# Four-layer graph network on one core: two of sixteen weight tiles of a unit move from VectorE to GpSimd

## The chip, the cores and the metric

The kernel runs on one core of a Trainium2 chip. A core has five engines with instruction queues of their own: TensorE (PE in the profile; its weight loads are PEld), VectorE (DVE), ScalarE (ACT), GpSimd (POOL) and SyncE (SP), which starts transfers. Each engine takes its instructions in order. SBUF is the working memory of 128 partitions, PSUM the memory in which TensorE leaves its sums.

The metric is the device time of one execution in microseconds (us). Before the change it is 1645.74, the median of 3 runs from 1645.39 to 1646.08.

## The reference, cut to what matters

The input is x (8 batches, N = 2048 nodes, 64 features) and one adjacency matrix of 2048 x 2048. Four layers follow, each x = layernorm(x + layer(x)). The first two are graph attention. For a batch, with h the projected features and s1, s2 two scores of every node:

```python
e = leaky_relu(s1[:, :, None] + s2[:, None, :], negative_slope=0.2)
att = softmax(where(adj > 0, e, very_small), axis=-1)
out = elu(matmul(att, h) [+ h in layer 0])
```

The third layer is the same with relu. The fourth takes a softmax along the neighbours for each feature.

A leaky relu is a maximum of two lines, and a factor that all weights of a row share drops out of a softmax. So in the first two layers the kernel needs no exponential of the 2048 x 2048 matrix. The weight of neighbour j for node i is, up to factors of i or of j alone, max(exp(0.8 s1[i]), exp(-0.8 s2[j])) times the mask; the factor exp(s2[j]) goes into the features of j.

## The kernel before

**Units.** A unit is one layer of one batch, named layer_batch. The first two layers run as 0_0 to 0_3, 1_0 to 1_3, 0_4 to 0_7, 1_4 to 1_7; then come the eight units of layer 2 (list `todo`, L1224). Layer 3 runs as background work.

**A unit's main loop** (L1297 to L1325) has K = 16 steps jb, one for each block of 128 neighbours. `attend` (L899) makes a weight tile w of 128 neighbours by 2048 nodes, and TensorE multiplies it in four chunks of 512 nodes with the features of that block, summing in the two PSUM tiles `acc`. In the first two layers the tile is one VectorE instruction, the maximum of a row and a scalar per partition, times the mask:

```python
dve.scalar_tensor_tensor(w, s.r, s.e[:, 1, jb : jb + 1], edge[:, jb, :], ALU.max, ALU.mult)
```

`edge` is the mask, 16 blocks of 128 x 2048 in fp8, kept in SBUF for the whole kernel. Tiles w share four buffers (tag "w").

**The row** s.r holds exp(0.8 s1) of all nodes, the same in each partition. Only unit 0_0 has it as f32 in SBUF. In the other 15 (`in_psum`, L566), `rows_term` (L569) splits the row on GpSimd into three bf16 pieces whose sum is the row (five small instructions on tile rT), writes them to DRAM, `prepare` (L724) loads them as r3, and `spread` (L744) has TensorE sum them into a PSUM tile r with four matmuls against ones. There is one such PSUM tile, so those matmuls come behind VectorE's last tile of the unit before. GpSimd does not read PSUM in this kernel.

**Background.** What a unit leaves to do, and what later units need, is written as generators (streams). After each step jb, `bg.step()` (L1325) takes every stream one step further; a stream says with the number that it yields how many steps it lets pass. Four of them matter here:
- `finish` (L937): ScalarE copies acc; TensorE multiplies it back to rows of nodes (p_o); VectorE takes the reciprocals of the sums (den); ScalarE scales (o); in layer 0 GpSimd adds hb; then eh and o on ScalarE and GpSimd (o<-o,eh is GpSimd's last sum), the statistics st_x (two VectorE reductions, and a power on GpSimd that takes isw_x to st_x), and x on ScalarE.
- `scores` (L677): from the new x to the scores of the next layer (p_xT, p_s), and the row.
- `features0` (L588): projection and layernorm of a batch for layer 0 (xs, p_h, st_h, y, h), and the row.
- `mean_pieces` (L552): the mean of all features in bf16 pieces, for nodes without neighbours, by small VectorE instructions (mean).

**Order.** The class InOrder (L68) keeps every engine in program order, the order in which Python writes the instructions. So a tile of the main loop and a background instruction written ahead of it on the same engine never change places, and an instruction that waits holds up all behind it. All such instructions carry line L78 in the profile; they are told apart by tile names. The buffers of a tag are handed out in the order in which they come free.

**The start.** Unit 0_0 also loads the adjacency matrix and makes the mask block by block (`load_raw`, L263; `mask`, L278). Eight of the blocks pass through buffers of tag "w", the others in halves through four buffers of tag "raw".

Of the kernel before, what the change touches and what calls it, by code (L numbers as in the profile page):

```python
# [8 lines left out]
F32 = mybir.dt.float32  # L9
BF16 = mybir.dt.bfloat16  # L10
U8 = mybir.dt.uint8
FP8 = mybir.dt.float8e4
I32 = mybir.dt.int32
AF = mybir.ActivationFunctionType
ALU = mybir.AluOpType
AX = mybir.AxisListType

P = 128
# [30 lines left out]
def gnn4_kernel(ctx: ExitStack, tc: tile.TileContext, t, out):  # L49
    nc = tc.nc  # L50
    x_in, adjT = t["x"], t["adjT"]
    B, N, F = x_in.shape
    K = N // P
# [8 lines left out]
    small = ctx.enter_context(tc.tile_pool(name="small", bufs=2))  # L62
    tmp = ctx.enter_context(tc.tile_pool(name="tmp", bufs=1))
    dram = ctx.enter_context(tc.tile_pool(name="dram", bufs=2, space=bass.MemoryType.DRAM))
# [40 lines left out]
    class Banks:  # L105
# [4 lines left out]
        pool = None  # L110
# [28 lines left out]
    pe, dve, act, pool = (InOrder(e) for e in (nc.tensor, nc.vector, nc.scalar, nc.gpsimd))  # L139
# [56 lines left out]
    work = ctx.enter_context(tc.tile_pool(name="work", bufs=2))  # L196
    early_ = ExitStack()
    early = early_.enter_context(tc.tile_pool(name="early", bufs=3))
# [49 lines left out]
    edge = consts.tile([P, K, N], FP8, name="edge")  # L248
# [14 lines left out]
    def load_raw(jb):  # L263

        if jb in AT_W:
            r = work.tile([P, N], I32, tag="w", name=f"raw_{jb}", bufs=4)
            nc.sync.dma_start(r, adjT[jb * P : (jb + 1) * P])
            raws[jb] = [r[:, : N // 2], r[:, N // 2 :]]
        elif jb < K:
            raws[jb] = []  # L270
            for h in range(2):
                r = early.tile([P, N // 2], I32, tag="raw", name=f"raw_{jb}_{h}", bufs=4)
                nc.sync.dma_start(
                    r, adjT[jb * P : (jb + 1) * P, h * (N // 2) : (h + 1) * (N // 2)]
                )
                raws[jb].append(r)
# [289 lines left out]
    def in_psum(layer, b):  # L566
        return layer < 2 and (layer, b) != (0, 0)

    def rows_term(sc, p, n, layer, b):  # L569

        if in_psum(layer, b):
            r = small.tile([K, P], F32, tag="rT", name=f"rT_{n}", bufs=1)
            act.copy(r, p)
            r3 = small.tile([K, 3, P], BF16, tag="rT3", name=f"rT3_{n}", bufs=1)
            for i in range(3):
                pool.tensor_copy(r3[:, i], r)
                if i < 2:
                    pool.tensor_tensor(r, r, r3[:, i], ALU.subtract)
            sc.row = dram.tile([3, K, P], BF16, tag="row3_d", name=f"row3_d_{n}", bufs=B + 1)
            nc.sync.dma_start(sc.row.rearrange("m k p -> k m p"), r3)  # L580
            return
        rT = small.tile([K, P], F32, tag="rT", name=f"rT_{n}", bufs=1)
        act.copy(rT, p)
        sc.row = dram.tile([K, P], F32, tag="row_d", name=f"row_d_{n}", bufs=B + 1)

        (nc.scalar if n == "0_0" else nc.sync).dma_start(sc.row, rT)
# [137 lines left out]
    def prepare(layer, b):  # L724

        n = f"{layer}_{b}"
        sc = S[layer, b]
        if in_psum(layer, b):
            sc.r3 = work.tile([P, 2 * N], BF16, tag="row", name=f"row3_{n}")[:3, :N]
            nc.sync.dma_start(sc.r3, sc.row.rearrange("m k p -> m (k p)"))  # L730
            sc.v = early.tile([P, K, F], F32, tag="pv", name=f"pv_{n}", bufs=2)
            pool.tensor_tensor(sc.v, V[layer, b].v, bc_f(sc.e[:, 2]), ALU.mult)
            return
        sc.r = work.tile([P, N], F32, tag="row", name=f"row_{n}")
        (nc.scalar if n == "0_0" else nc.sync).dma_start(
            sc.r, bass.AP(tensor=sc.row.tensor, offset=sc.row.offset, ap=[[0, P], [1, N]])
        )
        if layer < 2:
            sc.v = early.tile([P, K, F], F32, tag="pv", name=f"pv_{n}", bufs=2)
            pool.tensor_tensor(sc.v, V[layer, b].v, bc_f(sc.e[:, 2]), ALU.mult)  # L740
        else:
            sc.v = V[layer, b].v
# [147 lines left out]
    def exponential(b, chunk):  # L890
# [5 lines left out]
        )  # L896
        ahead[b, jb, c] = e

    def attend(u, jb, last):  # L899

        s = u.s
        if u.layer < 2:
            w = work.tile([P, N], F32, tag="w", name=f"w_{u.n}_{jb}", bufs=4)
            dve.scalar_tensor_tensor(
                w, s.r, s.e[:, 1, jb : jb + 1], edge[:, jb, :], ALU.max, ALU.mult
            )
        else:
            w = ahead[u.b, jb]
            if jb + 2 < K:
                clamp(u.layer, u.b, jb + 2)  # L910
            for c in range(2):
                sl = slice(c * 1024, (c + 1) * 1024)
                dve.tensor_tensor(w[:, sl], ahead[u.b, jb, c], edge[:, jb, sl], ALU.mult)
                chunk = 2 * jb + c + 2
                if chunk < 2 * K:
                    exponential(u.b, chunk)
                elif (u.b + 1, 0) in ahead:
                    exponential(u.b + 1, chunk - 2 * K)
        if jb == K - 1:
            last()  # L920
        sums = [u.acc[c // 2][F * (c % 2) : F * (c % 2) + F, :] for c in range(NCH)]
        for c in range(NCH):
            pe.matmul(
                sums[c],
                lhsT=s.v[:, jb, :],
                rhs=w[:, c * 512 : (c + 1) * 512],
                start=(jb == 0),
                stop=False,
            )
        if jb == K - 1:  # L930

            assert s.whole
            for c in range(NCH):
                rows = slice(32 * c, 32 * c + 3)
                pe.matmul(sums[c], lhsT=s.mean[rows], rhs=emptyT[rows], start=False, stop=True)
# [329 lines left out]
    for n, (layer, b) in enumerate(todo):  # L1265
        if (layer, b) == (2, 1):
            early_.close()
            late = ctx.enter_context(tc.tile_pool(name="late", bufs=1))
            bg.add(l3_products())
        if (layer, b) == (2, 5):  # L1270
            bg.add(flags())
        u = unit(layer, b)
        now[0] = layer
        nxt = todo[n + 1] if n + 1 < len(todo) else None
        done = nxt is None

        def first_exponentials():
            for chunk in range(2):
                if nxt is not None and nxt[0] == 2 and (nxt[1], 0) in ahead:
                    if (nxt[1], 0, chunk) not in ahead:  # L1280
                        exponential(nxt[1], chunk)

        def handover():

            if not done or nxt is None or S[nxt].__dict__.get("begun"):
                return
            if in_psum(*nxt):
                if n == 0:
                    Banks.use("psR", 1)
                spread(*nxt)  # L1290
            elif nxt == (2, 0):
                Banks.use("psE", 2)
                Banks.share()
            S[nxt].begun = True
            first_exponentials()

        for jb in range(K):  # L1297
            if n == 0:
                while masks < min(K, 9 + jb):
                    mask(p_deg, masks)  # L1300
                    masks += 1
                    if masks == K:
                        empties(p_deg)
            attend(u, jb, handover)
            if jb == K - 1:
                end = [lambda u=u: finish(u)]
                if layer < 2:
                    end += [2 if now[0] < 2 else 1, lambda layer=layer, b=b: scores(layer + 1, b)]
                else:
                    end += [1, lambda b=b: l3_features(b)]  # L1310
                if layer == 1 and b % NB == NB - 1:
                    end += [lambda b=b: group(b // NB)]
                bg.add(chain(*end), begun=True)
            elif not done and jb >= 10 and ready(*nxt):
                prepare(*nxt)
                done = True
            if done and nxt is not None and nxt[0] == 2 and jb >= K - 2:
                clamp(*nxt, jb - (K - 2))
            if layer == 0 and jb == 2 and 6 <= b + 4 < B:
                load_x(b + 4)  # L1320
            if n == 0 and jb == 3:
                bg.add(constants())
            if layer == 0 and jb == 4 and 2 <= b + 2 < B:
                bg.add(features0(b + 2))
            bg.step()  # L1325
        while not done:
            bg.step()
            if ready(*nxt):
                prepare(*nxt)
                done = True  # L1330
                if nxt[0] == 2:
                    clamp(*nxt, 0)
                    clamp(*nxt, 1)
        handover()
# [508 lines left out]
```

## Time and profile before

The span in the profile is 1643.8 us. Busy times of the whole span:

| engine | busy us | share |
|---|---|---|
| PE | 1349.0 | 82% |
| DVE | 1301.1 | 79% |
| ACT | 802.8 | 49% |
| POOL | 823.7 | 50% |
| PEld | 667.2 | 41% |

The 15 units in question run from 102.4 to 838.8 us. A line of a group reads: source line, engine, operation, output<-inputs, sizes, count | busy us, mean ns of one | idle time of the engine just before such instructions, and what ended it. A line of a timeline reads: start us, length us, engine, line, operation, output<-inputs, sizes, count, and in brackets the idle time before it and its releaser. "issue" means that the profile shows no wait. Instructions of one group that follow each other are merged, so `x4` with 9.10 us is four tiles.

### The profile page before, as it was taken

The numbers are of one execution on the slowest core, as the hardware profiler recorded it, in microseconds if no ns is written. First come the engines' busy times: TensorE is split into PE (matmuls) and PEld (weight loads), VectorE is DVE, ScalarE is ACT, GpSimd is POOL, SyncE is SP. The second block draws the span as 40 slices with busy tenths as digits, with TensorE's granted clock in tenths as the row PEclk, the third lists the DMA queues.
The fourth block names the chain that finished last, engine by engine and source line by source line (L and its number), as shares of the span: only waits on it lengthen the run. The fifth ranks groups of instructions, "written<-read, shape, count | busy, mean of one in ns | idle before, by whom it ended". The sixth has DMA issues, their size and how long they took to land.

```text
span 1643.8 us, 20952 instructions
## 1 busy us (share of the span) xinstructions
PE 1349.0 (82%) x8162; PEld 667.2 (41%) x8162; DVE 1301.1 (79%) x1334; ACT 802.8 (49%) x1635; POOL 823.7 (50%) x726
## 2 busy tenths in 40 slices
PE   3687879888888898888887676699896999587996
PEld 2222323333333343233322231165452545476885
DVE  4888877899887989898888878969897977738444
ACT  5234664443265443442378857676656664242111
POOL 2145353422222454321257748877789877546332
PEclk9999988899998999999999878899998999888998
DMA  8800000000000000000000000000010000000000
GB/s 329 215 5 1 1 2 1 1 2 1 1 1 2 1 2 2 2 1 26 26 1 26 26 1 27 0 26 8 30 33 7 4 4 11 10 4 14 11 14 19
DMA packets 42190, 36.86 MB, mean 22 GB/s; under 512 B 37509, under 2 KB 37813, under 8 KB 39906
## 3 DMA queue, kind: packets, MB, share of 16 engines
q1 hardware_dynamic: 41538, 34.26, 6.8%
q8 instruction: 66, 1.08, 0.3%
q10 hardware_dynamic: 544, 1.17, 0.2%
q14 instruction: 42, 0.34, 0.1%
HBM read 30.94 MB, written 4.45 MB: 22 GB/s over the span
## 4 chain that ended last, share of the span: by engine, by line
PE 31%; DVE 17%; ACT 7%; POOL 4%; issue 3%; POOLq 0%; DVEq 0%; ACTq 0%
PE p_l L78 18%; PE acc L78 11%; DVE w L78 10%; ACT e L78 3%; DVE o L78 2%; DVE st_x L78 2%; DVE x L78 1%; POOL v L78 1%; PE p_o L78 1%; ACT x L78 1%; POOL vf L78 1%; DVE f L78 1%; PE p_s L78 1%; POOL w L78 1%; POOL o L78 1%
## 5 line engine op out<-in xcount | busy, mean ns | idle before, releaser
L78 PE MATMUL acc<-w,pv 128*64 128x512 f32 x2048 | 525.4, 642 | 117.0 <-DVE w L78 95.1
L78 DVE SCALAR_TENSOR_TENSOR w<-r,se,edge 128x2048 f32<-128x2048 f32 x240 | 551.9, 2340 | 27.1 <-PE r L78 26.3
L78 PEld LDWEIGHTS <-edge 128*128 128x128 fp8e4 x3842 | 321.2, 99 | 153.1 <-issue 94.3
L78 PE MATMUL p_l<-v,edge 128*128 128x256 bf16 x3072 | 351.1, 275 | 37.4 <-ACT nd L78 13.1
L78 PE MATMUL acc<-w,x 128*64 128x512 f32 x1024 | 281.8, 667 | 87.4 <-DVE w L78 79.9
L78 ACT ACTIVATE e<-w,s_g 128x1024 f32<-128x1024 f32 x256 | 277.6, 1113 | 148.1 <-DVE w L78 103.7
L78 DVE TENSOR_TENSOR w<-e,edge 128x1024 f32<-128x1024 f32 x256 | 300.3, 1214 | 56.3 <-ACT e L78 54.2
L78 PEld LDWEIGHTS acc<-w,pv 128*64 128x64 f32 x2048 | 134.9, 143 | 401.6 <-issue 199.5
L78 POOL TENSOR_SCALAR w<-row,hi_g,lo_g 128x2048 f32<-128x2048 f32 x128 | 270.5, 2118 | 37.6 <-PE acc L78 33.4
L78 PEld LDWEIGHTS acc<-w,x 128*64 128x64 f32 x1024 | 64.0, 146 | 231.9 <-DVE w L78 154.7
L78 POOL TENSOR_TENSOR eh<-eh,x 128x1024 f32<-128x1024 f32 (+2 forms) x24 | 36.5, 1533 | 153.2 <-ACT eh L78 153.2
L78 ACT ACTIVATE nd<-p_l,empty 128x256 f32<-128x256 f32 x64 | 30.1, 470 | 158.8 <-PE p_l L78 158.8
L78 ACT ACTIVATE x<-o,st_x 128x64 f32<-128x64 f32 x256 | 87.4, 432 | 26.9 <-DVE st_x L78 26.9
L78 ACT COPY oT<-acc 128x512 f32<-128x512 f32 x48 | 25.7, 587 | 122.6 <-PE acc L78 122.5
L78 ACT ACTIVATE o<-p_o,den 128x64 f32<-128x64 f32 x256 | 56.2, 323 | 48.5 <-DVE den L78 48.4
L78 DVE RECIPROCAL den<-p_o 128x4 f32<-128x4 f32 x96 | 16.9, 179 | 73.5 <-PE p_o L78 59.5
L78 POOL TENSOR_TENSOR st_h<-isw_h,mhalf 128x16 f32<-128x16 f32 x8 | 23.6, 2956 | 99.2 <-DVE isw_h L78 94.9
L78 PEld LDWEIGHTS p_o<-rh,oT 128*128 128x128 f32 x384 | 51.2, 200 | 53.5 <-issue 32.0
L78 POOL TENSOR_TENSOR st_x<-isw_x,mhalf 128x16 f32<-128x16 f32 x24 | 70.5, 2936 | 2.0
L78 PE MATMUL p_o<-rh,oT 128*128 128x130 f32 x384 | 64.0, 302 | 7.9 <-ACT o L78 5.6
L78 POOL TENSOR_SCALAR isw<-isw 128x4 f32<-128x4 f32 x32 | 8.5, 265 | 122.6 <-DVE isw L78 122.5
L78 DVE TENSOR_REDUCE st<-sq 128x4 f32<-128x256 f32 x32 | 13.2, 414 | 70.4 <-ACT sq L78 70.3
(233 smaller groups left out, 1511.5 us busy)
## 6 DMA issues: line engine op xcount, KB each, us to landing
raw<-in_adjT_dram SPq DMA_DIRECT2D x8, 1024.0 KB
raw<-in_adjT_dram SPq DMA_DIRECT2D x16, 512.0 KB
row<-rows_d_g SPq DMA_DIRECT2D x8, 1024.0 KB
x<-in_x_dram SPq DMA_DIRECT2D x8, 512.0 KB
out_dram<-o SPq DMA_DIRECT2D x64, 64.0 KB
row<-row_d ACTq DMA_DIRECT2D x1, 1024.0 KB
row_d<-rT SPq DMA_DIRECT2D x15, 12.0 KB
row<-row_d SPq DMA_DIRECT2D x15, 12.0 KB
```

Of the source, the lines that this page charges most:

```text
L78: ins = f(*args, **kwargs)
```

## The change

In each of the 15 units, GpSimd makes the tiles 4 and 9 in place of VectorE, by a maximum and a product on each half of a tile. For this the change
- writes the f32 row to DRAM too (`sc.row1`) before it is split, and keeps the rest of the splitting in a tile of its own, rT1, so that the row isn't overwritten;
- loads that row into SBUF in `prepare`, in two halves that are the same in each partition (`sc.r1`);
- keeps bf16 copies of the mask blocks 4 and 9 (`wide`), made by VectorE after the last two steps of unit 0_0;
- renames the buffers of the half blocks: in place of four of tag "raw" two each of "half0" and "half1", which the row halves and the mask copies take over later;
- writes the tile three steps ahead: at jb = 1 tile 4, at jb = 6 tile 9, in the same four buffers of tag "w".

It is for taking work from VectorE to an engine that is busy for less of the span.

```diff
@@ load_raw
-                r = early.tile([P, N // 2], I32, tag="raw", name=f"raw_{jb}_{h}", bufs=4)
+                r = early.tile([P, N // 2], I32, tag=f"half{h}", name=f"raw_{jb}_{h}", bufs=2)
@@ rows_term
             act.copy(r, p)
+            sc.row1 = dram.tile([K, P], F32, tag="row_d", name=f"row_d_{n}", bufs=B + 1)
+            nc.sync.dma_start(sc.row1, r)
+            q = small.tile([K, P], F32, tag="rT1", name=f"rT1_{n}", bufs=1)
             r3 = small.tile([K, 3, P], BF16, tag="rT3", name=f"rT3_{n}", bufs=1)
             for i in range(3):
-                pool.tensor_copy(r3[:, i], r)
+                pool.tensor_copy(r3[:, i], q if i else r)
                 if i < 2:
-                    pool.tensor_tensor(r, r, r3[:, i], ALU.subtract)
+                    pool.tensor_tensor(q, q if i else r, r3[:, i], ALU.subtract)
@@ prepare
+            sc.r1 = []
+            for h in range(2):
+                r = early.tile([P, N // 2], F32, tag="half0", name=f"row1_{n}_{h}", bufs=2)
+                nc.sync.dma_start(
+                    r,
+                    bass.AP(
+                        tensor=sc.row1.tensor,
+                        offset=sc.row1.offset + h * (N // 2),
+                        ap=[[0, P], [1, N // 2]],
+                    ),
+                )
+                sc.r1.append(r)
@@ attend
+    BY_POOL = (4, 9)
+    wide = {}
+
+    def by_pool(u, jb, h):
+        s = u.s
+        if h == 0:
+            ahead[u.n, jb] = work.tile([P, N], F32, tag="w", name=f"w_{u.n}_{jb}", bufs=4)
+        sl = slice(h * (N // 2), (h + 1) * (N // 2))
+        w = ahead[u.n, jb][:, sl]
+        pool.tensor_scalar(w, s.r1[h], s.e[:, 1, jb : jb + 1], None, ALU.max)
+        pool.tensor_tensor(w, w, wide[jb][:, sl], ALU.mult)
+
     def attend(u, jb, last):
 
         s = u.s
-        if u.layer < 2:
+        if in_psum(u.layer, u.b) and jb + 3 in BY_POOL:
+            for h in range(2):
+                by_pool(u, jb + 3, h)
+        if (u.n, jb) in ahead:
+            w = ahead[u.n, jb]
+        elif u.layer < 2:
@@ main loop
             attend(u, jb, handover)
+            if n == 0 and jb >= K - 2:
+                j = BY_POOL[jb - (K - 2)]
+                wide[j] = early.tile([P, N], BF16, tag="half1", name=f"wide_{j}", bufs=2)
+                dve.tensor_copy(wide[j], edge[:, j])
```

## The prediction

> **What bounds the kernel now.** I read the page first. Its groups name the two costs that the change touches: the VectorE instruction that makes a weight tile, and the TensorE instructions that use it.
>
> ```profile
> L78 PE MATMUL acc<-w,pv 128*64 128x512 f32 x2048 | 525.4, 642 | 117.0 <-DVE w L78 95.1
> L78 DVE SCALAR_TENSOR_TENSOR w<-r,se,edge 128x2048 f32<-128x2048 f32 x240 | 551.9, 2340 | 27.1 <-PE r L78 26.3
> ```
>
> 240 tiles are 15 units of 16; a tile costs VectorE 2.34 us, and TensorE's idle time ahead of it is mostly a wait for VectorE (95.1 us of 117.0). Next I cut the trace into the 15 units that the change reaches (from the first r matmul of one to that of the next; 102.4 to 838.8 us) and asked for busy times by window. Columns: span, then busy us of PE, PEld, DVE, ACT, POOL, clock, DMA.
>
> ```profile
> 211.30:266.50 55.20, 45.29 (x189) 18.93 (x189) 44.96 (x35) 30.07 (x98) 22.64 (x23) 0.78 0.00 1
> 409.50:457.40 47.90, 40.28 (x181) 14.39 (x181) 40.89 (x27) 11.01 (x31) 9.58 (x6) 0.93 0.00 1
> 558.70:608.00 49.30, 47.94 (x441) 21.75 (x440) 42.08 (x35) 22.95 (x75) 26.10 (x25) 0.93 0.01 2
> sum 736.40, PE 625.27 PEld 239.70 DVE 633.18 ACT 326.03 POOL 257.69; mean PE 41.68 PEld 15.98 DVE 42.21 ACT 21.74 POOL 17.18
> ```
>
> A unit lasts 49.1 us on average with PE busy 41.7 and DVE 42.2: neither is the bound throughout. Which one ends a wait is seen in the instructions of one unit, 1_3 (409.5 to 457.4), DVE first, PE after it:
>
> ```profile
> 419.52 9.10 DVE L78 SCALAR_TENSOR_TENSOR w<-r,se,edge 128x2048 f32<-128x2048 f32 x4
> 432.23 0.18 DVE L78 RECIPROCAL den<-p_o 128x4 f32<-128x4 f32 x1 [3.61 <-issue]
> ...
> 437.27 1.26 DVE L78 SCALAR_TENSOR_TENSOR mean<-mean,later,mean 128x64 f32<-128x64 bf16 x1
> 438.45 4.60 DVE L78 SCALAR_TENSOR_TENSOR w<-r,se,edge 128x2048 f32<-128x2048 f32 x2
> 442.97 1.20 DVE L78 TENSOR_REDUCE st_x<-o 128x16 f32<-128x1024 f32 x1
> ```
>
> ```profile
> 426.14 5.35 PE L78 MATMUL acc<-w,pv 128*64 128x512 f32 x16
> 431.42 1.16 PE L78 MATMUL p_o<-rh,oT 128*128 128x130 f32 x8
> ...
> 440.84 1.94 PE L78 MATMUL acc<-w,pv 128*64 128x512 f32 x8 [1.50 <-DVE w L78]
> ...
> 446.48 1.94 PE L78 MATMUL acc<-w,pv 128*64 128x512 f32 x8 [1.45 <-DVE w L78]
> 450.36 7.07 PE L78 MATMUL acc<-w,pv 128*64 128x512 f32 x24 [1.94 <-DVE w L78]
> ```
>
> In the first half VectorE makes tiles 3 to 6, then stands 3.61 us in front of the reciprocal, whose p_o TensorE makes only at 431.42, after tiles 4 and 5: TensorE is late there. In the second half TensorE waits for tiles (1.50, 1.45, 1.94 us), so VectorE is late, up to tile 15 and the r matmul behind it. **Tile 4 lies in the half where VectorE has time to spare, tile 9 at the start of the half where it has none.**
>
> **What the Trainium skill says.** (1) "GPSIMD Engine Reference", 3.1: a two-input tensor_tensor of 2048 f32 takes 4497 ns on GpSimd, 1.96 times VectorE. The trace agrees: o<-o,eh, 1024 elements, takes 2361 ns. (2) "SBUF — State Buffer", "SBUF: two separate sides": VectorE (in a two-port mode, or with two SBUF inputs) and GpSimd take a shared port pair for a whole instruction, and the other blocks. The trace agrees on both sides. The mean instruction above takes 1.26 us beside eh<-eh,x; its usual time is 0.28. And in unit 0_0, whose row is in SBUF, tiny GpSimd instructions take the length of a tile:
>
> ```profile
> 93.34 0.28 POOL L78 CAST rT<-rT 16x128 bf16<-16x128 f32 x1
> 93.71 2.35 POOL L78 TENSOR_TENSOR rT<-rT,rT 16x128 f32<-16x128 f32 x1
> ```
>
> The tiles of the other 15 units read r from PSUM and so have one SBUF input: all 240 took 2315 to 2352 ns, whatever GpSimd did. So the big instructions won't collide with the new work; small ones will. (3) "VectorE: DVE Perf Modes", "Mode 2×_2P": a copy within SBUF can yield two elements a cycle; the wide copies have no row of their own, and the mask row (edge<-raw, 1024 elements in 689 ns) points the same way.
>
> **The change, part by part.** *Removed:* 2 x 2.34 = 4.68 us of VectorE a unit, 70.2 us in 15. *Added on GpSimd:* per tile, two halves of a max and a product. The max: clamp rows (w<-row,hi_g,lo_g) have median 2.05 us for 2048, so 1.02 a half. The product f32 x bf16: between 2.10 (vf<-vf,v, 4203 ns for 2048) and 2.36 (o<-o,eh). A tile is 6.2 to 6.8 us; I take 6.7, the high end, because the product has o<-o,eh's layout. That is 13.4 us a unit, 201 in all, on an engine busy 17.2 of 49.1: it fits as a sum, so the question is what queues behind it. *Added elsewhere:* one 8 KB write and two 512 KB loads a unit, hidden (the DMA engines are at 0.01, and the loads stand behind the r3 load that matters); 0_0's own 1 MB row held VectorE 10.1 us, and w4 is needed 20 us after the new load in 0_1. The renamed halves keep the four buffers. The f32 row q adds no instruction.
>
> *Order of the queues.* by_pool(4) is written at jb 1, by_pool(9) at jb 6, each ahead of what the streams add in the same step; how many steps a stream lets pass is the number that it yields, and GpSimd's order in the trace is the same. Buffers of tag w go round in the order in which they come free; with w4 and w9 written early, w4 waits for the unit before's w13, w9 for w2, w6 for w3, w7 for w4. By the times of before w9 can start when PE is through w2 (421.2 in 1_3) and be done 6.7 us later, well before 440.8; and PE is through w3 at 423.8, before VectorE would start w6. No tile is late for lack of a buffer.
>
> *Tile 4:* in 1_1, 1_2, 1_3, 1_4, 1_5, 1_6, 0_5, 0_6, 0_7 its 2.34 us become more idle time ahead of a reciprocal or of st_x<-o, whose input comes from TensorE, ScalarE and GpSimd: nothing. In 0_1 and 0_2 about 0.6 and 0.3. In 0_4 and 1_7 VectorE has no such wait left (1.1 us of slack), so part counts.
>
> *Tile 9:* I listed for every unit how long after VectorE ended a tile TensorE began it. Where that stays near 0.1 us from tile 10 to 15, TensorE has only its idle time to lose and the unit ends 2.3 us sooner, less what the reductions then wait. In 1_3 VectorE would be at st_x<-o at 440.6, but o<-o,eh ends at 441.06: 1.9. So: 1_1 2.3, 1_2 2.2, 1_3 1.9, 1_4 2.3, 1_5 2.3, 1_6 1.9 = 12.9. 0_4 and 1_7, both tiles, limited by the idle time that TensorE has from tile 4 on (2.8 and 3.7 us) and by the reduction: 2.5 + 2.8 = 5.3. 0_5 0.5, 1_0 0.5 (TensorE runs 3 us behind). With 0_1 and 0_2: 12.9 + 5.3 + 1.0 + 0.9 = **20.1 us gained**.
>
> *Delays behind GpSimd.* The queue is in program order, and VectorE waits for it in order:
>
> ```profile
> 592.40 1.22 DVE L78 TENSOR_REDUCE st_x<-o 128x16 f32<-128x1024 f32 x1 [3.49 <-POOL o L78]
> ```
>
> ```profile
> 590.01 2.35 POOL L78 TENSOR_TENSOR o<-o,eh 128x1024 f32<-128x1024 f32 x1
> ```
>
> In 0_6, by_pool(9) comes in after o<-o,hb (ends 578.8) and ends 585.5; the rT, h and eh instructions queue behind it and o<-o,eh ends 595.4, not 592.4: 3 us, of which TensorE's lag later takes 0.5. In 0_3 it falls between eh<-eh,x (ends 235.5) and o<-o,eh, which starts at 242.2, not 238.4; VectorE's next tile, for which TensorE already waited 4.31 us, comes 3 us later. In 0_7 eh<-eh,x waits 2.2, of which 0.9 arrives. In 1_2 and 1_5 the power of st_x ends some 2 us later and holds VectorE 0.6 and 0.5. Sum 2.5 + 3.0 + 0.9 + 1.1 = **7.5 us lost**.
>
> *The shared port.* I laid the 6.7 us windows over VectorE's small instructions with two SBUF inputs: 14 meetings, 6 of them in the half that VectorE sets. A meeting costs on average what is left of a GpSimd instruction: (1.02² + 2.36²)/(2 x 3.38) = 0.98, say 0.9 us; **5.4 us lost**.
>
> *The wide copies:* two in 0_0, before the first tile of 0_1. 1.3 us each from the mask row, at most a tile's 2.34; 0.79 and 1.19 us of idle time follow. 0.6 to 2.7; I take **1.0 us**.
>
> Net 20.1 - 7.5 - 5.4 - 1.0 = 6.2 us: 1645.7 - 6.2 = **1639.5**.
>
> **The rivals.** *GpSimd's queue becomes the bound* (slower). Then a product or two stands ahead of a chain in all eight units that finish a first-layer unit (0_1, 0_2, 0_3, 1_0, 0_5, 0_6, 0_7, 1_4), 3 us each as in 0_6, 24 in all; and of the 8 meetings in the first halves half count too, 5.4 + 4 x 0.98 = 9.3. With the copies 24 + 9.3 + 1.0 - 20.1 = +14: 1660. For it: 78% more work on a queue that VectorE waits for in order. Against: in 1_1, 1_2, 1_3, 1_5 and 1_6 GpSimd stands idle 15 to 33 us at a time ahead of eh, and in 0_1 and 0_2 13 to 23 us. *Washed out:* gain and delays cancel, 1645. *VectorE was the bound after all:* both tiles count, down to TensorE's floor. VectorE then gives 70 us, less the reciprocals' waits in the first halves, about half: 1611. For it: the 95.1 us wait; against: 3.61 us of idle VectorE right behind tile 6.
>
> **How the numbers follow.** Forecast 0.48, slower rival 0.30, washed out 0.14, both tiles 0.08. Faster is forecast plus both tiles, with a little taken off because 6 us is near 3.3: 0.55. Slower 0.32, within 0.2% 0.13. The range must leave out most of the extremes: from 1624 (the 20.1 us without any loss) to 1660 (the middle of the slower rival).
>
> **What would show it.** Right: GpSimd busy 257.7 + 201 us in these units; TensorE's wait for VectorE's w shorter in second halves; reciprocals waiting longer by tile 4; o<-o,eh about 3 us later in 0_3 and 0_6. Wrong: big VectorE tiles longer than 2352 ns; GpSimd's halves over 3.4 us; TensorE waiting for w from POOL, which would mean that a buffer or the row came late; or a reduction waiting for POOL o in units where I put no delay.

## The result, and the profile after

The changed kernel takes **1674.71 us**, the median of four runs (1673.27 to 1676.72), against 1645.57 us before (1644.35 to 1646.08). The ratio is 1.0179, with a 95% interval from 1.0161 to 1.0197: slower by 1.8%, where 0.4% faster was forecast, and above the range of 1624 to 1660.

The group of the matmuls on the page of the changed kernel, whose line of before the prediction shows:

```profile
L78 PE MATMUL acc<-w,pv 128*64 128x512 f32 x2048 | 526.3, 647 | 144.1 <-DVE w L78 118.1
```

The tiles and the new work, in the groups of the changed kernel with different shapes kept apart:

```profile
L78 DVE SCALAR_TENSOR_TENSOR w<-r,se,edge 128x2048 f32<-128x2048 f32 x210 | 483.9, 2338 | 25.9 <-PE r L78 23.6 <-PE acc L78 2.3
L78 POOL TENSOR_SCALAR w<-row,hi_g,lo_g 128x2048 f32<-128x2048 f32 x128 | 269.9, 2114 | 36.2 <-PE acc L78 27.3 <-issue 2.5 <-DVE vf L78 2.4
L78 POOL TENSOR_SCALAR w<-row,se 128x1024 f32<-128x1024 f32 x60 | 170.6, 2843 | 23.8 <-PE acc L78 23.7
L78 POOL TENSOR_TENSOR w<-w,wide 128x1024 f32<-128x1024 f32 x60 | 128.0, 2133 | 5.0
L78 DVE TENSOR_REDUCE st_x<-o 128x16 f32<-128x1024 f32 x24 | 29.2, 1215 | 60.0 <-POOL o L78 60.0
```

VectorE lost 30 tiles, as meant, and each remaining tile keeps its length (2338 ns, 2340 before). The product takes 2133 ns, inside the bounds of the prediction. The max (w<-row,se) takes **2843 ns for half a tile**; 1020 had been assumed. The clamp in the second line, which does two operations and handles twice the elements, takes 2114. A tile thus costs GpSimd 2 x (2.84 + 2.13) = 9.95 us instead of 6.7, and TensorE's idle time behind VectorE's w rose from 95.1 to 118.1 us where it should have fallen.

The last line says where the tiles' work arrives. The first reduction of a layernorm waits 60.0 us for GpSimd's o. In the waits (who waits for whom: total us, times, longest) of before the same wait is small:

```profile
DVE st_x L78 <- POOL o L78: 10.7, 6, 3.6
```

After the change:

```profile
DVE st_x L78 <- POOL o L78: 60.0, 14, 12.3
```

Unit 0_6 holds the longest. It starts at 571.9 us in the trace of the changed kernel. On GpSimd:

```profile
590.69 2.37 POOL L78 TENSOR_TENSOR o<-o,hb 128x1024 f32<-128x1024 f32 x1 [1.93 <-ACT o L78]
593.04 2.84 POOL L78 TENSOR_SCALAR w<-row,se 128x1024 f32<-128x1024 f32 x1
595.96 2.14 POOL L78 TENSOR_TENSOR w<-w,wide 128x1024 f32<-128x1024 f32 x1
598.07 2.85 POOL L78 TENSOR_SCALAR w<-row,se 128x1024 f32<-128x1024 f32 x1
601.01 2.13 POOL L78 TENSOR_TENSOR w<-w,wide 128x1024 f32<-128x1024 f32 x1
...
608.40 2.34 POOL L78 TENSOR_TENSOR eh<-eh,x 128x1024 f32<-128x1024 f32 x1
610.82 2.34 POOL L78 TENSOR_TENSOR o<-o,eh 128x1024 f32<-128x1024 f32 x1
```

On VectorE, and below it on TensorE, in the same stretch:

```profile
589.56 11.36 DVE L78 SCALAR_TENSOR_TENSOR w<-r,se,edge 128x2048 f32<-128x2048 f32 x5
613.19 1.22 DVE L78 TENSOR_REDUCE st_x<-o 128x16 f32<-128x1024 f32 x1 [12.27 <-POOL o L78]
614.33 2.34 DVE L78 SCALAR_TENSOR_TENSOR w<-r,se,edge 128x2048 f32<-128x2048 f32 x1
```

```profile
616.73 5.65 PE L78 MATMUL acc<-w,pv 128*64 128x512 f32 x12 [6.65 <-DVE w L78]
```

Tile 9 is ready at 603.1 and late for nobody. But the 10 us that it takes stand in GpSimd's queue ahead of eh and o. VectorE, after five tiles in one piece, stands 12.27 us in front of the reduction, and behind that reduction stands its next tile, for which TensorE then waits 6.65 us. o<-o,eh ends 41.2 us after the start of the unit, 33.7 before the change.

Cut at the start of each unit, the 15 units took 736.4 us before and 765.3 after, +28.9, which is nearly the whole difference. The largest losses are in 0_6 (+7.8), 0_7 (+6.9), 1_0 (+4.9), 1_5 (+3.5) and 1_2 (+3.4). Units 1_3, 1_6 and 1_1 gained 3.6, 1.9 and 0.6.

### The profile page after: what moved, and what is told of

Its sections match the earlier page's. It is cut to its first block, busy times and chain, and to the rows that moved or that the text cites. A ratio compares the mean times of both kernels' runs of the same rounds, so it can differ in the third digit from the quotient of the medians.

```text
span 1672.5 us, 21160 instructions
## 1 busy us (share of the span) xinstructions
PE 1348.2 (81%) x8162; PEld 667.9 (40%) x8162; DVE 1260.5 (75%) x1306; ACT 801.6 (48%) x1635; POOL 1121.0 (67%) x846
## 4 chain that ended last, share of the span: by engine, by line
PE 29%; DVE 15%; ACT 8%; POOL 7%; issue 3%; POOLq 0%; DVEq 0%; ACTq 0%
PE p_l L78 17%; PE acc L78 10%; DVE w L78 8%; ACT e L78 3%; POOL w L78 2%; DVE o L78 2%; DVE st_x L78 1%; POOL o L78 1%; DVE x L78 1%; POOL v L78 1%; ACT x L78 1%; PE p_o L78 1%; POOL vf L78 1%; ACT o L78 1%; POOL st_x L78 1%
## 5 line engine op out<-in xcount | busy, mean ns | idle before, releaser
L78 PE MATMUL acc<-w,pv 128*64 128x512 f32 x2048 | 526.3, 647 | 144.1 <-DVE w L78 118.1
L78 DVE SCALAR_TENSOR_TENSOR w<-r,se,edge 128x2048 f32<-128x2048 f32 x210 | 483.9, 2338 | 25.9 <-PE r L78 23.6
L78 POOL TENSOR_SCALAR w<-row,se 128x1024 f32<-128x1024 f32 x60 | 170.6, 2843 | 23.8 <-PE acc L78 23.7
L78 POOL TENSOR_TENSOR w<-w,wide 128x1024 f32<-128x1024 f32 x60 | 128.0, 2133 | 5.0
L78 DVE TENSOR_REDUCE st_x<-o 128x16 f32<-128x1024 f32 x24 | 29.2, 1215 | 60.0 <-POOL o L78 60.0
```

The lines of the kernel that those rows point to most:

```text
L78: ins = f(*args, **kwargs)
```

## The experiments

All ratios are against the kernel before on the same chip (1647.2 to 1648.0 us). "In us" means (ratio - 1) x 1645.6, the interval in the same way.

**1. Does the length of the max set the time?** Three kernels have the same 60 halves in the same places and differ only in how long a half's max takes. One repeats the max:

```diff
-        pool.tensor_scalar(w, s.r1[h], s.e[:, 1, jb : jb + 1], None, ALU.max)
+        k = s.e[:, 1, jb : jb + 1]
+        pool.tensor_scalar(w, s.r1[h], k, k, ALU.max, ALU.max)
```

> The maximum is written with two operations (max, max with the same scalar) like the clamp of layer 2 (min, max), nothing else changes. Theory (one operation per element was mis-sized: 2.84 us a half where I took 1.02): if the two-operation form runs like the clamp, a half takes 1.0 to 1.1 us, a tile 6.3 instead of 9.95, and the time comes to about what the prediction worked out, 1636 to 1650. Rival (the place in GpSimd's queue or the shared port costs the time, whatever a tile's length): above 1662. If the form is as slow as before, 1675 and nothing is learned but that.

It took 1707.8 us, ratio 1.0369 (1.0351 to 1.0387). The other puts a minimum with 3e38 ahead of the max, which changes no value, so that the instruction has the form of the clamp; `big` is a column of 3e38:

```diff
-        pool.tensor_scalar(w, s.r1[h], s.e[:, 1, jb : jb + 1], None, ALU.max)
+        k = s.e[:, 1, jb : jb + 1]
+        pool.tensor_scalar(w, s.r1[h], big, k, ALU.min, ALU.max)
```

> The maximum written exactly as the clamp of layer 2: minimum with a large number per partition, then maximum with the scalar. All else as in the change. If this form takes what the clamp takes, a half is 1.0 to 1.1 us and a tile 6.3 us, which is what the prediction assumed. Theory (the length of the maximum is the term that failed): 1630 to 1648. Rival (the place in the queue and the shared port cost the time, not the length): 1660 or more, since count and place of the instructions are the same.

It took 1649.27 us, ratio 1.0010 (0.9998 to 1.0022), which its interval does not tell from no change. Groups of the kernel with the max twice:

```profile
L78 POOL TENSOR_SCALAR w<-row,se 128x1024 f32<-128x1024 f32 x60 | 226.5, 3776 | 20.6 <-PE acc L78 20.5
```

and of the one with min and max:

```profile
L78 POOL TENSOR_SCALAR w<-row,big,se 128x1024 f32<-128x1024 f32 x60 | 71.8, 1196 | 38.0 <-PE acc L78 38.0
L78 POOL TENSOR_TENSOR w<-w,wide 128x1024 f32<-128x1024 f32 x60 | 128.0, 2133 | 5.0
L78 DVE TENSOR_REDUCE st_x<-o 128x16 f32<-128x1024 f32 x24 | 29.2, 1215 | 42.2 <-POOL o L78 42.2
```

A half's max of 1.20, 2.84 and 3.78 us gives 1.6, 29.5 and 60.7 us over before, and the reductions wait 42.2, 60.0 and 74.4 us for GpSimd's o. The length of this one instruction is worth 27.9 us of the 29.5. With min and max a tile costs 6.66 us, the 6.7 of the prediction; the time is still 1.6 us over before and not 6.2 under it. So a second part of the prediction failed too.

**2. The gain without the load.** On the kernel before, with none of the change in it, tiles 4 and 9 are made by nobody; TensorE multiplies a constant tile, made once, in their place.

```diff
+        if in_psum(u.layer, u.b) and jb in (4, 9):
+            w = None
...
-                rhs=w[:, c * 512 : (c + 1) * 512],
+                rhs=(
+                    fixed[c // 2][:, c % 2 * 512 : c % 2 * 512 + 512]
+                    if w is None
+                    else w[:, c * 512 : (c + 1) * 512]
+                ),
```

> Nobody makes tiles 4 and 9 in the 15 units: TensorE multiplies a constant tile (the sum of two mask blocks, made once) in their place, and nothing of the change is in it, so its output leaves these weights out. It shows what freeing VectorE of 30 tiles is worth without any cost on GpSimd. Theory: 20 us, 1620 to 1630. Rival (VectorE is off the path, so that the gain was overestimated): 1638 or more. Rival (both tiles count everywhere): 1605 or less.

1616.06 us, ratio 0.9815 (0.9794 to 0.9836): 30.4 us (27 to 34) are gained where 20.1 were forecast. The gain was sized too small; it is not the step that made the change slow.

**3. The load without the gain.** VectorE makes all sixteen tiles, and GpSimd does the same work, at the same places of its queue, in place on the row halves, where nobody reads it:

```diff
-        if h == 0:
-            ahead[u.n, jb] = work.tile([P, N], F32, tag="w", name=f"w_{u.n}_{jb}", bufs=4)
...
-        w = ahead[u.n, jb][:, sl]
+        w = s.r1[h]
```

> The reverse: VectorE makes all 16 tiles, and GpSimd does the same work at the same places of its queue, in place on the row halves, which nobody reads. It shows the cost of GpSimd's load alone. Theory: the loss of 29 us is cost less gain, so the load alone costs 29 + 20, about 1685 to 1700. Rival (TensorE waits for late tiles from GpSimd or for their buffers): at most 1655, since nobody waits for these results.

1699.73 us, ratio 1.0319 (1.0301 to 1.0337), 52.5 us. The same with the short max:

> GpSimd's load alone with the short maximum: VectorE makes all 16 tiles, GpSimd works in place on the row halves. With the long maximum this cost 52 us. If the cost goes with GpSimd's busy time: 52 x 6.3 / 9.95 = 33 us, 1679. If it goes with the part that sticks out of GpSimd's idle stretches, as the theory has it, clearly less: 1655 to 1668. If the length does not matter (rival): 1695.

1665.79 us, ratio 1.0110 (1.0081 to 1.0139), 18.1 us. Both slow the kernel without moving one tile. Last, the load without its reads. For each tile GpSimd writes the row halves seven times (the first half three times, the second four times) and reads nothing:

```diff
-        pool.tensor_scalar(w, s.r1[h], s.e[:, 1, jb : jb + 1], None, ALU.max)
-        pool.tensor_tensor(w, w, wide[jb][:, sl], ALU.mult)
+        w = s.r1[h]
+        for _ in range(3 + h):
+            pool.memset(w, 1.0)
```

> VectorE makes all 16 tiles; in place of the two by_pool calls of a unit GpSimd does seven memsets of 1024 elements each on the row halves, about 6.6 us at the same places of its queue, so as long as the short maximum and product, but reading nothing. The load that read SBUF cost 18 us alone, and made VectorE's small instructions 14 us longer in sum. If the shared port is what counts (small instructions with two SBUF inputs blocked by GpSimd's reads): 1648 to 1656, with the small instructions near their 41 us of before. If the queue behind it is what counts: 1662 to 1670, as with reads. Both: between.

The seven writes stand in place of each tile, not of both tiles of a unit as the text above has it. So there are 210 of them, and they are as long together as the work that they replace: 198.0 us, against 71.9 + 128.0 = 199.9 with reads. The groups of the kernel without reads:

```profile
L78 POOL MEMSET row<- 128x1024 f32 x210 | 198.0, 952 | 8.6
L78 DVE SCALAR_TENSOR_TENSOR mean<-mean,later,mean 128x64 f32<-128x64 bf16 x48 | 19.8, 415 | 3.3 <-ACT mean L78 3.3
L78 DVE SCALAR_TENSOR_TENSOR isw_x<-st_x 128x16 f32<-128x16 f32 x24 | 9.4, 393 | 0.0
L78 DVE SCALAR_TENSOR_TENSOR isw_x<-st_x,isw_x 128x16 f32<-128x16 f32 x24 | 4.2, 175 | 0.8
```

and of the one with reads and the short max:

```profile
L78 POOL TENSOR_SCALAR row<-row,big,se 128x1024 f32<-128x1024 f32 x60 | 71.9, 1198 | 0.0
L78 POOL TENSOR_TENSOR row<-row,wide 128x1024 f32<-128x1024 f32 x60 | 128.0, 2134 | 5.0
L78 DVE SCALAR_TENSOR_TENSOR mean<-mean,later,mean 128x64 f32<-128x64 bf16 x48 | 25.2, 528 | 3.3 <-ACT mean L78 3.3
L78 DVE SCALAR_TENSOR_TENSOR isw_x<-st_x 128x16 f32<-128x16 f32 x24 | 13.4, 559 | 0.0
L78 DVE SCALAR_TENSOR_TENSOR isw_x<-st_x,isw_x 128x16 f32<-128x16 f32 x24 | 6.1, 254 | 0.8
```

It took 1655.55 us, ratio 1.0048 (1.0032 to 1.0065), 7.9 us. The reads cost the other 10.2 us (18.1 - 7.9; by the two intervals, 5 to 16). The lines show how: the same small VectorE instructions are longer when GpSimd reads SBUF. isw_x<-st_x has a mean of 559 ns with reads and 393 without, which is the 392 of the kernel before. All small VectorE instructions of the 15 units (without tiles, reductions, reciprocals and the wide copies) sum to 55.5 us with reads, 41.8 without and 41.3 before. This is what the Trainium skill says ("SBUF — State Buffer", "SBUF: two separate sides"): a GpSimd operation that reads SBUF and a VectorE operation with two SBUF inputs hold each other up. The big tiles, whose r lies in PSUM, were free of it in every kernel (2312 to 2353 ns).

**4. One tile alone.** Tile 9 alone, with the long max (only one mask copy is made then, here and in the kernels below with one tile):

```diff
-    BY_POOL = (4, 9)
+    BY_POOL = (9,)
```

> GpSimd makes tile 9 alone, with the maximum as in the change, and VectorE makes tile 4. Theory (tile 4's removal is worth next to nothing, tile 9's up to 13 us and more, but by_pool(9) is what stands ahead of the eh and o sums): about 1650 to 1665. Rival (the load counts as a sum, half of it for half the tiles): 1660. Rival (by_pool(4) is the costly one): below 1645.

1668.4 us, ratio 1.0126 (1.0107 to 1.0145), 20.7 us, more than was expected. With the short max:

> Tile 9 alone, with the short maximum. Theory (tile 9 holds most of the gain, and its work comes behind fewer other things): 1628 to 1642, at or below the run with both tiles and the short maximum. Rival (each tile is worth the same): halfway between before and the run with both.

1633.88 us, ratio 0.9911 (0.9879 to 0.9943), a gain of 14.6 us. Tile 4 alone, with the short max:

> Tile 4 alone with the short maximum. The prediction gave its removal from VectorE about nothing in eleven units. Theory: it costs and brings little, 1647 to 1658, so that with tile 9's 1634 the two add up to the 1649 of both. Rival (each tile is worth the same): 1634.

1641.98 us, ratio 0.9969 (0.9946 to 0.9991), a gain of 5.1 us. Together the two gain nothing (+1.6): 21 us less than their sum. Tile 4 is not nearly worthless, as had been forecast, but its gain is lost when tile 9 goes to GpSimd as well. For tile 9 alone the long max costs 35.3 us more than the short one (20.7 + 14.6, ±6), no less than the 27.9 for both tiles. So the long max does most of its harm at tile 9; tile 4 alone was not run with it.

**5. Tile 9 ahead of the chain.** As in 4, with the short max, but tile 9 written at jb = 1, five steps sooner, so that it stands in GpSimd's queue ahead of the sums with hb and eh:

```diff
-        if in_psum(u.layer, u.b) and jb + 3 in BY_POOL:
+        if in_psum(u.layer, u.b) and jb == 1:
             for h in range(2):
-                by_pool(u, jb + 3, h)
+                by_pool(u, 9, h)
```

> Tile 9 alone with the short maximum, written at jb 1 and not at jb 6, so that it stands ahead of the eh and o sums in every unit, at the price of a buffer held longer. Theory (what stands ahead of o<-o,eh costs the time): 5 us or more below the run with tile 9 at jb 6, 1622 to 1630. Rival (a buffer held for eight tiles makes VectorE wait): above it, 1636 or more.

1625.05 us, ratio 0.9862 (0.9839 to 0.9885), a gain of 22.7 us. Waits and groups of this kernel:

```profile
DVE st_x L78 <- POOL o L78: 18.2, 9, 5.7
```

```profile
L78 POOL TENSOR_SCALAR w<-row,big,se 128x1024 f32<-128x1024 f32 x30 | 35.9, 1196 | 14.2 <-PE acc L78 14.1
```

and of tile 9 at jb = 6:

```profile
DVE st_x L78 <- POOL o L78: 29.3, 10, 9.0
```

```profile
L78 POOL TENSOR_SCALAR w<-row,big,se 128x1024 f32<-128x1024 f32 x30 | 35.7, 1190 | 53.0 <-PE acc L78 53.0
```

The same work, 30 tiles of the same length, is worth 8.1 us more (±6.5) where it stands ahead of the chain's sums. The reductions wait 11.1 us less. GpSimd itself also waits 39 us less for a buffer of tag "w" to be read out by TensorE. That wait is not what costs the time, as the kernel with tile 9 at jb = 6 shows. Its 53.0 us are four waits, and behind each of these tiles GpSimd stands idle again, for 0.3, 6.5, 6.6 and 8.3 us, because the next instruction's input isn't there yet. Unit 1_3:

```profile
419.62 1.19 POOL L78 TENSOR_SCALAR w<-row,big,se 128x1024 f32<-128x1024 f32 x1 [17.55 <-PE acc L78]
...
433.01 2.18 POOL L78 TENSOR_TENSOR eh<-eh,x 128x1008 f32<-128x1008 f32 x2 [6.59 <-ACT eh L78]
```

eh<-eh,x would not have started sooner without the wait for a buffer.

**6. The mask without copies.** The product reads the fp8 mask itself, and the wide copies go. With both tiles and the short max:

```diff
-        pool.tensor_tensor(w, w, wide[jb][:, sl], ALU.mult)
+        pool.tensor_tensor(w, w, edge[:, jb, sl], ALU.mult)
...
-            if n == 0 and jb >= K - 2:
-                j = BY_POOL[jb - (K - 2)]
-                wide[j] = early.tile([P, N], BF16, tag="half1", name=f"wide_{j}", bufs=2)
-                dve.tensor_copy(wide[j], edge[:, j])
```

> As the run with both tiles and the short maximum, but the product reads the fp8 mask itself, so that the two wide copies fall away (3.5 us of VectorE ahead of 0_1). If an fp8 operand costs GpSimd nothing, 1 to 4 us below that run; if it makes the product longer (over 2.5 us), above it.

1644.89 us, ratio 0.9976 (0.9965 to 0.9988), a gain of 3.9 us, 5.5 better than with the copies. How much of that is the copies and how much the shorter products was not separated. The product with fp8:

```profile
L78 POOL TENSOR_TENSOR w<-w,edge 128x1024 f32<-128x1024 f32 x60 | 120.8, 2013 | 5.0
```

Put together, tile 9 alone, short max, written at jb = 1, fp8 mask:

> As the run with tile 9 at jb 1, with the product reading the fp8 mask and no wide copy. The copies cost the run with both tiles about 4 us. Theory: one copy less, about 2 us below: 1620 to 1628.

**1620.11 us** (1618.1 to 1623.97), ratio 0.9828 (0.9812 to 0.9845). It is faster than both kernels, by 1.7% than the one before and by 3.4% than the changed one (0.9828 / 1.0179). By the ratios it comes within 2.1 us of the kernel in which nobody makes the two tiles, a difference that the intervals cover.

## Why the prediction was wrong

The sum of the prediction beside what the runs gave for the same terms (us, minus is faster):

| term | forecast | measured | from |
|---|---|---|---|
| gain of the two tiles | -20.1 | -30.4 (±3.5) | tiles made by nobody |
| queue behind GpSimd, wide copies, row loads | +7.5 + 1.0 | +7.9 (±2.7) | load without reads |
| shared port | +5.4 | +10.2 (±5.5) | load with reads less that without |
| tiles and load together, beyond their sum | 0 | +13.9 (±6) | short max, 1.6, less -30.4 and 18.1 |
| max longer than assumed | 0 | +27.9 (±3.6) | 29.5 less 1.6 |
| sum | -6.2 | +29.5 (±3) | |

**The step that failed** is "The max: clamp rows (w<-row,hi_g,lo_g) have median 2.05 us for 2048, so 1.02 a half". The max took 2.84 us a half. The price came from the nearest row, an instruction of the same engine, name and operand, but with another pair of operations. The step gave no upper bound for it, though the product was bounded from both sides. The slowest row of that size that the prediction used, o<-o,eh with 2.36 us for a half, would have given 9.4 us a tile: a warning, though still below the 9.95 measured. The short max shows that this step failed: same kernel, same places, 1.20 us a half, and 27.9 us are gone.

**The gain** had the right mechanism and too small a size. Tile 4 was put at nothing in nine units because VectorE stands in front of a reciprocal there. On its own, its load included, it gains 5.1 us (1.5 to 8.9), so probably not all of those 2.34 us end in front of a reciprocal. In the trace of the kernel in which nobody makes the tiles, the units that gain most beyond the forecast are 1_1 (6.9 us for 2.3), 1_0 (3.7 for 0.5), 0_5 (2.8 for 0.5), 1_4 (4.2 for 2.3) and 1_3 (3.7 for 1.9). In 1_1, o<-o,eh ends 4.6 us sooner in the unit than before, in 0_5 2.0 and in 1_3 1.7: the prediction had left this sum where it was, as a limit to the gain. How much of the 10.3 us missing is tile 4's and how much tile 9's was not measured without load.

**The queue** was right as a mechanism, and with work of the assumed length it cost as much in sum as was forecast (7.9 for 8.5). That the sums agree is in part luck: in the trace of the load without reads, 0_3, 0_6 and 0_7 are 2.7, 4.1 and 0.8 us longer than before (3.0, 2.5 and 0.9 had been forecast), but 1_0 is 3.2 longer and 0_5 is 4.0 shorter, and for neither was anything forecast. In the changed kernel, where the chain was said to be held, it is held: in 0_6 and in 0_3, where o<-o,eh ends 7.5 and 5.9 us later in the unit than before, and in 0_7 (8.4). In 1_0, 0_5 and 1_4, where the prediction put no delay, it is 8.8, 5.5 and 3.0; a reduction waiting for GpSimd's o in 1_0 (8.7 us) was one of its signs of being wrong. **The port** cost about twice the forecast. The prediction counted 14 meetings of some 0.9 us. Of the 134 small instructions in the units, 24 last over 0.7 us with the load alone and the short max, 10 before, and their sum rises by 14.2 us (55.5 from 41.3). So count and size were about right; too small was the share of 6 in 14 that was let count.

**Together.** Even with the short max, the parts measured singly sum to -12.3, and the kernel has +1.6. The prediction had put this term at nothing by adding gain and losses. Where the 13.9 us go, the traces show only in part. The reductions wait 42.2 us for o with both, 26.5 with the gain alone, 23.7 with the load alone and 10.7 before. The single rises, 15.8 and 13.0, already give nearly the whole rise of 31.5, so only 2.7 us of the loss lie there. Ahead of the reciprocals of the 15 units VectorE stands idle for 59.7 us with both, against 56.9, 41.7 and 49.4: here both together cost 10.5 us more than the sum. GpSimd waits 38.0 us for buffers, which the load alone doesn't, as it fills no tile. But as in experiment 5, behind each of these tiles it stands idle again, for 0.3 us or more, before the next instruction that isn't a tile, so no chain is held by that wait. No tile is late either (TensorE never waits for a w of GpSimd with the short max, and 4.9 us in all in the changed kernel). That VectorE, relieved, comes earlier to a reciprocal whose input comes no earlier fits these lines and was not tested. Each line is of one execution, and in these four executions the units show 6.5 us beyond the sum. So how the 13.9 us divide stays open.

**Of the rivals**, "GpSimd's queue becomes the bound" was right in direction. Its products stand ahead of the chains as it said, but at 10 us a tile and not 6.7, so its 1660 fell short. This was in part luck: with the 6.66 us of the short max the kernel is at +1.6 and not at the rival's +14, nearest to "washed out". What made the kernel slow is the price of the max, which is in no rival's sum. The rival gave a sign to look for, "GpSimd's halves over 3.4 us", and that is what the trace shows (4.98). GpSimd's busy time in the units rose by 297 us (257.7 to 554.8), not by 201. **The rest held:** tiles of 2340 ns, a product of 2.13 us, transfers hidden, no tile late for want of the row. The wide copies took 1.23 and 2.29 us; what they cost was not measured. The first unit starts 1.5 us later than before, but in the two kernels without copies that have the rest of the change it starts 2.7 and 4.0 us later, so its start moves for other reasons.

## What to carry to other kernels

When a change moves work to an engine that the trace shows with other operations, bound each instruction's length from both sides, and ask how the answer changes if the worst holds: here one instruction's price was most of the result. Work that nobody waits for still costs what stands behind it in a queue in program order, so write it ahead of the chain and not in front of the chain's last links. A wait in such a queue costs only if what stands behind it was ready, so look at the next instruction's own wait before you count it. Measure the gain (work made by nobody) and the load (work used by nobody) apart, and don't trust their sum.

## What the runs showed of the hardware that was not expected

- On GpSimd a max of 128x1024 f32 with one scalar per partition takes 2.84 us, and with two maxima 3.78, so the second adds 0.93. A min followed by a max takes 1.20. One instruction that does more is 2.4 times as fast. The Trainium skill ("GPSIMD Engine Reference", 4.1 "Engine selection") calls one-input work on GpSimd "roughly line-rate". The measurement decides, and for the max alone it differs: 2.84 us is longer than the product with two inputs, 2.13. Why the pair is faster was not tested.
- The product of f32 with fp8 takes 2.01 us for 128x1024, with bf16 2.13. A product of two f32 (hb<-y,L_gnn_ln_gamma_bc, 128x1008 in the kernel before) takes 2.33. In these three rows the narrower second operand goes with the shorter product; the third also repeats its second operand, so its layout differs.
- GpSimd writes 128x1024 f32 in 0.95 us, and such writes left VectorE's small instructions at their usual length (41.8 us in sum, 41.3 before).
